# Layer two of a graph network: whole-block contexts for blocks 0 to 11, the maximum and the residual behind GpSimd's offset, half contexts for blocks 12 to 15

## The chip, the cores and the metric

The kernel runs on one core of one Trainium2 chip. The time is device microseconds for one execution, the median of several runs. Lower is better. In the text PE is TensorE (PEld its weight load), DVE is VectorE, ACT is ScalarE, POOL is GpSimd and SP is SyncE, whose queue issues the DMAs.

## The reference

Two graph layers over 128 graphs of 64 nodes with 768 features, in fp32. For one layer, with h the rows of one graph:

```
u[i,j] = h_i . (W_left h_j) for j >= i, h_i . (W_right h_j) for j < i, over sqrt(768)
att = exp(u) * adj / (row sum + 1e-10)
ctx = att @ (h @ W_lin^T + b)
h   = relu((ctx - mean) / (std(ddof=1) + 1e-3) * a + b)
```

Before layer one, h = relu(layernorm(x)); after layer two the result is x + h. What matters here is the end of layer two: the context `ctx`, its deviation, the scale by 1/(std + eps) and the row `a` (the mean is already out of it, since the weights are centred), the offset `b`, the maximum with zero, and the sum with `x`.

## The kernel before, in words

The 8192 rows are 16 blocks of 512 (8 graphs each). Each layer has two passes. Pass one (`pass_one`) makes the attention of all blocks and stores it. Pass two (`pass_two`) goes over the blocks u = 0 to 15 again: `linear(u, ...)` makes `hl` = h W_lin of block u, and the context of block u-1 is made in the midst of it, one block behind.

`linear` is a fast matrix multiplication: 15 products instead of 18 (the list `ORDER`, i = 0 to 14). For a product PE does eight matmuls of 128x256 with weights `W[l, "n"]` and a sum of token chunks; the result goes into one of four PSUM banks X, Y, Z, V. After each product the bank is added into `hl`: what comes to an `hl` part first is copied by ACT (L305), the others are added by DVE (L223). A bank that is used again has to be read out first: X takes i = 0, 2, 4, 6, 8, 10, Y takes 3, 7, 11, Z takes 1, 13, V takes 5, 9, 12, 14. `fresh` lets ACT put a bias into X, Y or V ahead of i = 0, 3, 5, 9 (L843, `AHEAD` holds the X of the next block). The eleven token sums of block u+1 (`T_SUMS`: ta, u1, u2, u0, u3, td, tb, te, tc, tg, tf) are made on POOL during block u (L223, output `ts`), from `ht` of u+1, which SP loads (`load_h`, L375) and ACT brings to relu(a h + b) in six pieces (`affine`, L382).

Everything that isn't in `ORDER` is put into numbered slots of the block by hand: `put(n, f)`. Slot 2i runs in the middle of product i, slot 2i+1 after it and after its reading; slots of 30 and more run in the next block, 30 lower. A slot sets the place of an instruction in the queue of its engine, nothing else: every engine works through its own queue in order. So `affine` stands at slots 9 to 14, the token sums at 15 to 19, 21 to 25 and 27.

The context of layer two before the change is done in halves: `finish(u, r)` for r = 0, 1, called from `linear` where `ends` names a product. It does

- `context(u, r)` (L877): 16 matmuls of 64x384 on the four 64x64 quarters of PE, into two PSUM tiles `aux` of two banks each,
- ACT: two squares with a sum (L1022) and one root (L1024),
- `inverse` (DVE, L1027 and L1028), then for each of two tiles `scaled` (DVE, L1032: context times 1/std times the row `a`; then POOL, L1035: plus the row `b`) and `done` (DVE, L1046: maximum with zero, plus `x` in the tile `xr`; two stores to the output on SP, L1048). After the second tile `residual` loads the `x` of a coming half (SP, L962).

In layer two before, `ends` puts the half (u-1, 0) behind product 0 and (u-1, 1) behind product 7 of block u, for u = 1 to 14, with the steps at slots 6, 7, 8, 11, 12 and 20, 21, 22, 30, 30. Block 15 runs as two half passes with an own placing, and `finish_last` ends the program.

In layer one (L900) most contexts are done by whole blocks: `finish_block` behind product 12. `context_block(u)` does 32 matmuls: for each of four tiles, 512 columns into a bank and 256 into another. The 512 columns of (1,1) and (1,0) go into X and Y, the rest into `aux`. As X and Y are needed again, DVE copies them into the tile `z` (L972). After that come eight squares (L983), one root for four tiles (L987, L988), the inverse (L991, L992) and the scaling on ACT (L997).

Of the kernel before, what the change touches and what calls it, by code (L numbers as in the profile page):

```python
# [13 lines left out]
ALU = mybir.AluOpType  # L14
# [3 lines left out]
def kernel(  # L18
# [12 lines left out]
    nc = tc.nc  # L31
# [33 lines left out]
    def put(slot, *fs):  # L65
        plan.setdefault(slot, []).extend(fs)
# [780 lines left out]
    def pass_two(l, aside):  # L847
        last = l == L - 1
        with (tc.tile_pool(name=f"ps_two{l}", bufs=1, space=bass.MemoryType.PSUM) as ps,
# [108 lines left out]
            def residual(u, r):  # L958
                XS[u, r] = [sp.tile([P, H], F32, name="xr", bufs=4) for _ in range(2)]
                for k in range(2):  # L960
                    for h in range(PAIR):
                        nc.sync.dma_start(XS[u, r][k][h * S:(h + 1) * S], x[u * NBB + batch(r, k, h)])  # L962

            def finish_block(u, more):

                parts = context_block(u)
                tiles = ((0, 0), (0, 1), (1, 0), (1, 1))
                zs = {t: sp.tile([P, H], F32, name="z", bufs=4) for t in tiles}
                cut = (slice(0, T), slice(T, H))

                for t in ((1, 1), (1, 0)):
                    nc.vector.tensor_copy(zs[t][:, cut[0]], parts[t][0])  # L972
                    parts[t][0] = zs[t][:, cut[0]]
                    if t == (1, 1):
                        AHEAD.append(fresh(l, 0, more))
                ss = stat.tile([P, Q, 2], F32, name="ssb", bufs=2)
                sd = stat.tile([P, Q], F32, name="sdb", bufs=2)
                rs = stat.tile([P, Q], F32, name="rsb", bufs=2)

                def squares(t):  # L980
                    junk = zs[0, t[1]]
                    for n in range(2):
                        nc.scalar.activation(junk[:, cut[n]], parts[t][n], AF.Square,  # L983
                                             accum_out=ss[:, 2 * t[0] + t[1], n:n + 1])

                def deviation():
                    nc.vector.reduce_sum(sd, ss, axis=mybir.AxisListType.X)  # L987
                    nc.scalar.activation(sd, sd, AF.Sqrt, bias=floor, scale=1.0 / (H - 1.0))  # L988

                def inverse():  # L990
                    nc.vector.tensor_scalar_add(rs, sd, EPS_LN)  # L991
                    nc.vector.reciprocal(rs, rs)  # L992

                def scaled(t):
                    by = rs[:, 2 * t[0] + t[1]:2 * t[0] + t[1] + 1]
                    for n in range(2):
                        nc.scalar.activation(zs[t][:, cut[n]], parts[t][n], AF.Copy, scale=by)  # L997
                    kept(u, *t, zs[t])

                order = ((1, 1), (1, 0), (0, 0), (0, 1))  # L1000
                for f, slots in ((squares, (25, 26, 28, 29)), (scaled, (33, 34, 35, 36))):
                    for n, t in zip(slots, order):
                        put(n, lambda f=f, t=t: f(t))
                put(30, deviation)
                put(32, inverse)

            def kept(u, r, k, z):
                for h in range(PAIR):
# [2 lines left out]
            def finish(u, r):  # L1011

                cx = context(u, r)
                zs = [sp.tile([P, H], F32, name="z", bufs=4) for _ in range(2)]
                if last and not u and not r:
                    residual(u, r)
                two = "p (n d) -> p n d"
                ss = stat.tile([P, 2], F32, name="ss", bufs=2)
                sd = stat.tile([P, 2], F32, name="sd1", bufs=2)
                rs = stat.tile([P, 2], F32, name="rs1", bufs=2)  # L1020
                for k in range(2):
                    nc.scalar.activation(zs[k].rearrange(two, n=2), cx[k], AF.Square, accum_out=ss[:, k:k + 1])  # L1022

                nc.scalar.activation(sd, ss, AF.Sqrt, bias=floor, scale=1.0 / (H - 1.0))  # L1024

                def inverse():
                    nc.vector.tensor_scalar_add(rs, sd, EPS_LN)  # L1027
                    nc.vector.reciprocal(rs, rs)  # L1028

                def scaled(k):  # L1030
                    if last:
                        nc.vector.scalar_tensor_tensor(  # L1032
                            zs[k].rearrange(two, n=2), cx[k], rs[:, k:k + 1],
                            rows["a"].rearrange(two, n=2), op0=ALU.mult, op1=ALU.mult)
                        nc.gpsimd.tensor_add(zs[k], zs[k], rows["b"])  # L1035
                        return
                    if (u, r, k) == (NB - 1, 1, 1):
                        nc.vector.tensor_scalar_mul(zs[k].rearrange(two, n=2), cx[k], rs[:, k:k + 1])
                    else:
                        nc.scalar.activation(zs[k].rearrange(two, n=2), cx[k], AF.Copy, scale=rs[:, k:k + 1])  # L1040
                    kept(u, r, k, zs[k])

                def done(k):
                    if last:
                        xs = XS[u, r]
                        nc.vector.scalar_tensor_tensor(xs[k], zs[k], 0.0, xs[k], op0=ALU.max, op1=ALU.add)  # L1046
                        for h in range(PAIR):
                            nc.sync.dma_start(out[u * NBB + batch(r, k, h)], xs[k][h * S:(h + 1) * S])  # L1048
                        if k and u + r < NB - 1 and (u, r) != (NB - 2, 0):
                            residual(u + r, 1 - r)  # L1050

                steps = [lambda f=f, k=k: f(k) for f in (scaled, done) for k in range(2)]
                return [inverse] + (steps if last else steps[:2])

# [37 lines left out]
            for u in range(NB):  # L1092
                turn = not last and u >= NB - 2
                put(4, lambda u=u: load_at(u))
                if u + 1 < NB:
                    if u:
                        load_h(2, l, u + 1)
                        put_all(9, affine(2, l, u + 1))
                    put_sums_t((2, l, u + 1), 15 if u else 21, 1, 0)
                    if not last and NB - 5 <= u < NB - 3:  # L1100
                        load_rows(1, u + 5 - NB, sp)
                        put_all(14, transpose_rows(1, u + 5 - NB, sp), 2)
                    if not last and u >= NB - 3:
                        put(2, lambda u=u: load_h(1, 1, u + 3 - NB))
                        put_all(21 if u == NB - 3 else 11, affine(1, 1, u + 3 - NB), 1 if u == NB - 3 else 3)
                    if u in aside:
                        aside[u]()
                    ends = {}
                    if u and last:
                        ends = {0: ((u - 1, 0), (6, 7, 8, 11, 12)), 7: ((u - 1, 1), (20, 21, 22, 30, 30))}  # L1110
                    elif u > NB - 3:
                        ends = {5: ((u - 1, 0), (16, 17, 18)), 11: ((u - 1, 1), (28, 29, 30))}
                    elif u:
                        ends = {12: (u - 1, None)}
                    linear(u, (0, 1), 0, ends, (0, 1) if u + 2 < NB else (0,))
                    for n in sorted(plan):
                        plan[n - 30] = plan.pop(n)
                else:
                    if turn:
                        put_token_ops(1, 0, "before")  # L1120
                        assert not idle, len(idle)
                        for n in range(RINGS - 1):
                            put(20 + 4 * n, lambda n=n: stream(1, n))
                        ends = ({1: ((u - 1, 0), (13, 14, 16)), 11: ((u - 1, 1), (34, 35, 36))},
                                {4: ((u, 0), (50, 51, 52))})
                    else:
                        last_block(u)
                        put(8, lambda: residual(u - 1, 1))
                        ends = ({0: ((u - 1, 0), (12, 13, 15, 19, 31)), 9: ((u - 1, 1), (28, 29, 30, 39, 41))},
                                {2: ((u, 0), (44, 48, 51, 61, 62))})  # L1130
                    linear(u, (0,), 0, ends[0], (1,))
                    linear(u, (1,), 30, ends[1], ())
                    for n in sorted(plan):
                        run(n)
                    for f in (finish_last if last else finish)(u, 1):
                        f()
# [72 lines left out]
```

## Time and profile before

| what | value |
|---|---|
| median of three runs | 2707.16 us (2706.79 to 2707.33) |
| the profiled execution, its own time | 2705.84 us |
| its span, first to last instruction | 2704.1 us |
| time around the span | 1.74 us |
| granted TensorE clock, mean | 0.998 |
| PE busy over the span | 2677.7 us |
| layer two, pass two, from its first product to the last context | 2223.75 to 2690.95 us |
| PE, DVE, ACT, POOL busy in one block of it (2454.94 to 2484.14, 29.20 us) | 29.20, 19.87, 13.68, 23.64 us |

In the profile, a line of the timeline gives start, duration, engine, source line, operation, tiles and count; in brackets the idle time before it and what ended it. The matmuls overlap: eight of 128x256 begin 1.727 us before the next eight. In the table by form, the numbers behind the bar are the busy time of the group and the mean time of one in ns. Times of POOL are rough.

### The profile page before, as it was taken

What the parts mean: (1) busy time and instruction counts of PE and PEld (TensorE: products, weight loads), DVE (VectorE), ACT (ScalarE), POOL (GpSimd) and SP (SyncE); (2) the same over time, 40 slices, a digit from 0 to 9 for tenths busy, and PEclk for the clock granted to TensorE, in tenths of its full rate; (3) what the DMA queues carried; (4) which work ended last, traced back from release to release, by engine and by line L of the source; (5) the groups of instructions that cost most, each with busy time, mean ns of one, the idle gap of its engine ahead of it and who ended that gap; (6) DMA issues with size and microseconds to landing.
All of it is one profiled execution on the core that took longest, in us unless ns stands there. A gap on an engine that the chain in (4) does not pass through costs nothing.

```text
span 2704.1 us, 47306 instructions
## 1 busy us (share of the span) xinstructions
PE 2677.7 (99%) x18514; PEld 2301.3 (85%) x18514; DVE 1499.1 (55%) x2456; ACT 832.4 (31%) x1617; POOL 1381.4 (51%) x1071
## 2 busy tenths in 40 slices
PE   9999999999999999999999999999999999999998
PEld 8788888888888888888788888888888888888886
DVE  7664755756647433334344545546446475666667
ACT  4032131221310254454631221221212304445443
POOL 6633244333336765566433325335244286887886
PEclk9999999999999999999999999999999999999999
DMA  8886956858765345558594956968759524655655
GB/s 272 268 309 212 289 197 208 279 202 265 244 207 181 102 143 184 166 167 255 184 284 174 317 187 212 286 191 279 229 193 301 211 79 135 182 160 159 186 154 148
DMA packets 310222, 567.81 MB, mean 210 GB/s; under 512 B 62832, under 2 KB 190064, under 8 KB 301808
## 3 DMA queue, kind: packets, MB, share of 16 engines
q1 hardware_dynamic: 309840, 564.39, 64.9%
q8 instruction: 148, 2.42, 0.4%
q14 instruction: 74, 0.61, 0.1%
q10 hardware_dynamic: 160, 0.39, 0.0%
HBM read 429.40 MB, written 135.27 MB: 209 GB/s over the span
## 4 chain that ended last, share of the span: by engine, by line
PE 96%; DVE 1%; SPq 0%; issue 0%; DMA 0%; ACT 0%; DVEq 0%; ACTq 0%
PE right L535 17%; PE X L1069 12%; PE X L535 11%; PE V L535 11%; PE Z L535 9%; PE Y L535 9%; PE V L1069 8%; PE Y L1069 6%; PE both L474 5%; PE Z L1069 4%; PE aux L877 2%; PE aux L900 1%; PE Y L900 0%; PE Z L474 0%; DVE wp L223 0%
## 5 line engine op out<-in xcount | busy, mean ns | idle before, releaser
L223 POOL TENSOR_TENSOR ts<-ht 128x512 f32<-128x512 f32 x352 | 481.6, 1374 | 172.6 <-PE X L1069 69.6
L223 POOL TENSOR_TENSOR ts<-ht,ts 128x512 f32<-128x512 f32 x192 | 252.9, 1324 | 345.7 <-PE V L535 202.1
L535 PE MATMUL right<-ts,wp 128*128 128x252 f32 (+1 forms) x1632 | 380.9, 376 | 0.6 <-DVE wp L223 0.6
L535 PEld LDWEIGHTS right<-ts,wp 128*128 128x128 f32 x1632 | 310.0, 190 | 39.5 <-DVE wp L223 1.0
L483 POOL TENSOR_TENSOR wm<-adj,tri 128x256 f32<-128x256 f32 x60 | 42.3, 728 | 490.7 <-DMA wp<-ws 274.5
L223 DVE TENSOR_TENSOR m<-m,X 128x512 f32<-128x512 f32 x160 | 105.5, 684 | 257.9 <-ACT m L305 180.2
L223 DVE TENSOR_TENSOR m<-m,right 128x504 f32<-128x504 f32 (+1 forms) x304 | 199.5, 674 | 87.8 <-PE right L535 74.1
L1069 PE MATMUL X<-room,ts 128*128 128x256 f32 x1024 | 244.0, 380 | 0.2
L535 PE MATMUL Z<-ts,wp 128*128 128x256 f32 x992 | 234.3, 379 | 0.0
L223 POOL TENSOR_TENSOR ts<-ht,ht 128x512 f32<-128x512 f32 x128 | 163.2, 1285 | 137.8 <-PE right L535 92.8
L1069 PEld LDWEIGHTS X<-room,ts 128*128 128x128 f32 x1024 | 191.7, 190 | 31.7 <-issue 1.8
L535 PEld LDWEIGHTS Z<-ts,wp 128*128 128x128 f32 x992 | 188.4, 190 | 24.9
L535 PE MATMUL X<-ts,wp 128*128 128x256 f32 x872 | 207.5, 381 | 1.9 <-DVE wp L223 1.9
L535 PE MATMUL V<-ts,wp 128*128 128x252 f32 (+1 forms) x864 | 201.6, 376 | 0.0
L305 ACT ACTIVATE m<-right 128x504 f32<-128x504 f32 (+1 forms) x64 | 36.2, 592 | 506.8 <-PE both L474 486.8
L535 PEld LDWEIGHTS X<-ts,wp 128*128 128x128 f32 x872 | 164.4, 190 | 25.5 <-POOL ts L223 2.3
L382 ACT ACTIVATE ht<-ht,b_col,a_col 128x512 f32<-128x512 f32 x192 | 141.3, 806 | 140.9 <-DMA ht<-h 140.9
L1069 PE MATMUL Y<-room,ts 128*128 128x256 f32 x768 | 182.5, 379 | 0.0
L535 PEld LDWEIGHTS V<-ts,wp 128*128 128x128 f32 x864 | 164.2, 190 | 20.4
L1069 PEld LDWEIGHTS Y<-room,ts 128*128 128x128 f32 x768 | 145.8, 190 | 20.4 <-issue 0.6
L223 DVE TENSOR_TENSOR hl<-hl,V 128x512 f32<-128x512 f32 (+1 forms) x136 | 89.2, 656 | 128.9 <-PE V L1069 118.7
L223 DVE TENSOR_TENSOR m<-m,Y 128x512 f32<-128x512 f32 x144 | 95.8, 684 | 116.0 <-PE Y L535 105.2
(225 smaller groups left out, 4866.3 us busy)
## 6 DMA issues: line engine op xcount, KB each, us to landing
wp<-ws SPq DMA_DIRECT2D x435, 512.0 KB, 6.3
ht<-h SPq DMA_DIRECT2D x62, 1536.0 KB, 8.3
h<-room SPq DMA_DIRECT2D x112, 384.0 KB, 7.1
z<-z SPq DMA_DIRECT2D x128, 192.0 KB, 3.1
ws<-wp SPq DMA_DIRECT2D x93, 256.0 KB, 4.2
xr<-in_x_dram SPq DMA_DIRECT2D x120, 192.0 KB, 3.6
out_dram<-xr SPq DMA_DIRECT2D x120, 192.0 KB, 2.6
room<-z SPq DMA_DIRECT2D x112, 192.0 KB, 5.1
```

Of the source, the lines that this page charges most:

```text
L223: (eng.tensor_add if sign == "+" else eng.tensor_sub)(o, a, b)
L305: nc.scalar.activation(to(o), p, AF.Copy, scale=1.0 if sign == "+" else -1.0)
L382: nc.scalar.activation(ht, ht, AF.Relu, bias=cols[1][:, c:c + 1], scale=cols[0][:, c:c + 1])
L474: nc.tensor.matmul(p[h * S + e:h * S + e + 32, q, e:e + 95], ht[:, c, b * S + e:b * S + e + 32], mb[:, e:e + 95], start=(c == 0), stop=(c ...
L483: nc.gpsimd.tensor_tensor(wm[:, :, k], adj[:, :, 1 - k], tri[:, k].unsqueeze(1).to_broadcast([P, Q, S]), op=ALU.mult)
L535: nc.tensor.matmul(p[:, g], wk[:, c, g * P:(g + 1) * P], tk[:, c, :].rearrange("p (b s) -> p b s", s=S)[:, :, :ns], start=(new and g == c ...
L877: nc.tensor.matmul(cx[k][i, m, :HH], at[j, q, :], hl[j, q, m * HH:(m + 1) * HH], start=True, stop=True)
L900: nc.tensor.matmul(parts[r, k][n][i], at[j, q, :], hl[j, q, cut], start=True, stop=True)
L1069: nc.tensor.matmul(p[:, n], b[t][:, c, r * P:(r + 1) * P], w[s][:, c, :], start=(i in FIRST and i not in PRELOAD and n == c == 0), stop=(c ...
```

## The change

`finish_block` now serves layer two as well. For u = 1 to 12 `ends` is {12: (u-1, None)}, so that blocks 0 to 11 get a whole-block context behind product 12. In the last layer its steps differ from those of layer one: Y is copied by ACT, not DVE; the scaling is done by DVE in two parts for each tile, with the row `a` (slots 33 to 36, in the next block 3 to 6), and POOL adds `b` to the whole tile; the maximum and the residual, now a function `added_rows`, have slots of their own, 39, 42, 44, 47 (in the next block 9, 12, 14, 17); the `x` of the next block is loaded by `residual` for both halves at slot 48 (18). For block 0 it is loaded at slot 20.

Blocks 12 to 15 keep half contexts. (12,0) and (12,1) move to behind products 9 and 14 of block 13, (13,0) and (13,1) to behind products 5 and 11 of block 14. Block 15 is as it was.

```diff
--- before.py
+++ after.py
@@ -969,7 +969,7 @@
                 cut = (slice(0, T), slice(T, H))
 
                 for t in ((1, 1), (1, 0)):
-                    nc.vector.tensor_copy(zs[t][:, cut[0]], parts[t][0])
+                    (nc.scalar.copy if last and t == (1, 0) else nc.vector.tensor_copy)(zs[t][:, cut[0]], parts[t][0])
                     parts[t][0] = zs[t][:, cut[0]]
                     if t == (1, 1):
                         AHEAD.append(fresh(l, 0, more))
@@ -993,17 +993,34 @@
 
                 def scaled(t):
                     by = rs[:, 2 * t[0] + t[1]:2 * t[0] + t[1] + 1]
+                    if last:
+                        for n in range(2):
+                            nc.vector.scalar_tensor_tensor(zs[t][:, cut[n]], parts[t][n], by, rows["a"][:, cut[n]],
+                                                           op0=ALU.mult, op1=ALU.mult)
+                        nc.gpsimd.tensor_add(zs[t], zs[t], rows["b"])
+                        return
                     for n in range(2):
                         nc.scalar.activation(zs[t][:, cut[n]], parts[t][n], AF.Copy, scale=by)
                     kept(u, *t, zs[t])
 
                 order = ((1, 1), (1, 0), (0, 0), (0, 1))
-                for f, slots in ((squares, (25, 26, 28, 29)), (scaled, (33, 34, 35, 36))):
+                steps = [(squares, (25, 26, 28, 29)), (scaled, (33, 34, 35, 36))]
+                if last:
+                    steps.append((lambda t: added_rows(u, *t, zs[t]), (39, 42, 44, 47)))
+                    for r in range(2):
+                        put(48, lambda r=r: residual(u + 1, r))
+                for f, slots in steps:
                     for n, t in zip(slots, order):
                         put(n, lambda f=f, t=t: f(t))
                 put(30, deviation)
                 put(32, inverse)
 
+            def added_rows(u, r, k, z):
+                xs = XS[u, r][k]
+                nc.vector.scalar_tensor_tensor(xs, z, 0.0, xs, op0=ALU.max, op1=ALU.add)
+                for h in range(PAIR):
+                    nc.sync.dma_start(out[u * NBB + batch(r, k, h)], xs[h * S:(h + 1) * S])
+
             def kept(u, r, k, z):
                 for h in range(PAIR):
                     nc.sync.dma_start(ROWS[u][batch(r, k, h)], z[h * S:(h + 1) * S])
@@ -1012,8 +1029,6 @@
 
                 cx = context(u, r)
                 zs = [sp.tile([P, H], F32, name="z", bufs=4) for _ in range(2)]
-                if last and not u and not r:
-                    residual(u, r)
                 two = "p (n d) -> p n d"
                 ss = stat.tile([P, 2], F32, name="ss", bufs=2)
                 sd = stat.tile([P, 2], F32, name="sd1", bufs=2)
@@ -1042,11 +1057,8 @@
 
                 def done(k):
                     if last:
-                        xs = XS[u, r]
-                        nc.vector.scalar_tensor_tensor(xs[k], zs[k], 0.0, xs[k], op0=ALU.max, op1=ALU.add)
-                        for h in range(PAIR):
-                            nc.sync.dma_start(out[u * NBB + batch(r, k, h)], xs[k][h * S:(h + 1) * S])
-                        if k and u + r < NB - 1 and (u, r) != (NB - 2, 0):
+                        added_rows(u, r, k, zs[k])
+                        if k and u + r < NB - 1 and (u, r) not in ((NB - 4, 0), (NB - 2, 0)):
                             residual(u + r, 1 - r)
 
                 steps = [lambda f=f, k=k: f(k) for f in (scaled, done) for k in range(2)]
@@ -1106,8 +1118,12 @@
                     if u in aside:
                         aside[u]()
                     ends = {}
-                    if u and last:
-                        ends = {0: ((u - 1, 0), (6, 7, 8, 11, 12)), 7: ((u - 1, 1), (20, 21, 22, 30, 30))}
+                    if last and not u:
+                        for r in range(2):
+                            put(20, lambda r=r: residual(0, r))
+                    if last and u > NB - 4:
+                        ends = ({9: ((u - 1, 0), (24, 25, 26, 29, 30)), 14: ((u - 1, 1), (34, 35, 36, 39, 40))},
+                                {5: ((u - 1, 0), (16, 17, 18, 21, 22)), 11: ((u - 1, 1), (28, 29, 30, 33, 34))})[u + 3 - NB]
                     elif u > NB - 3:
                         ends = {5: ((u - 1, 0), (16, 17, 18)), 11: ((u - 1, 1), (28, 29, 30))}
                     elif u:
```

## The prediction

> **What bounds the kernel now.** I read the busy times and the chain of the page first, then PE's timeline over one block of each layer's second pass, the busy time of each engine in one block, DVE's groups by form, and at last the few stretches where DVE and POOL work at once.
>
> ```profile
> PE 2677.7 (99%) x18514; PEld 2301.3 (85%) x18514; DVE 1499.1 (55%) x2456; ACT 832.4 (31%) x1617; POOL 1381.4 (51%) x1071
> ...
> PE 96%; DVE 1%; SPq 0%; issue 0%; DMA 0%; ACT 0%; DVEq 0%; ACTq 0%
> ```
>
> PE is the bound: work moved off another engine gains nothing; what counts is PE's own time and new waits of PE. One block of layer two (first fence) holds two half contexts, one of layer one (second) a whole one:
>
> ```profile
> 2454.94 1.89 PE L1069 MATMUL X<-room,ts 128*128 128x256 f32 x8
> 2456.76 1.52 PE L877 MATMUL aux<-hl,at 64*64 64x384 f32 x16
> 2458.21 1.99 PE L1069 MATMUL Z<-room,ts 128*128 128x256 f32 x8
> ...
> 2470.50 1.52 PE L877 MATMUL aux<-hl,at 64*64 64x384 f32 x16
> 2471.95 1.99 PE L1069 MATMUL X<-room,ht 128*128 128x256 f32 x8
> 2473.78 1.89 PE L1069 MATMUL V<-room,ht 128*128 128x256 f32 x8
> 2475.50 1.89 PE L1069 MATMUL X<-room,ts 128*128 128x256 f32 x8
> ```
>
> ```profile
> 1054.41 1.89 PE L1069 MATMUL V<-room,ts 128*128 128x256 f32 x8
> ...
> 1057.14 1.90 PE L900 MATMUL aux<-hl,at 64*64 64x256 f32 x24
> ```
>
> Products follow at 1.727 us (2473.78 to 2475.50). Layer two's block runs from 2454.94 to the next X at 2484.14: 29.20 us, no bracket with a wait. So a half costs (29.20 - 15 x 1.727) / 2 = 1.65 us. In layer one the product behind the context starts at 1030.14, one block later at 1058.97: 28.84 us with the third digit, so a whole context costs 2.94.
>
> **The gain.** Two halves 3.30, one whole 2.94: 0.36 us a block, for 12 blocks **-4.3 us**. The columns are the same (16 x 384 = 8 x 512 + 8 x 256, twice); one entry and exit less is the difference. The other edits can only lose.
>
> **The steady block (u = 2 to 12).** PE starts product i at t = 1.727 i up to 12, the context at 22.5, the next block at 28.84. A read by DVE starts 0.27 after its product. Prices:
>
> ```profile
> L1046 DVE SCALAR_TENSOR_TENSOR xr<-z,xr 128x768 f32<-128x768 f32 x48 | 91.0, 1933 | 0.0
> L1032 DVE SCALAR_TENSOR_TENSOR z<-aux,rs,a 128x768 f32<-128x768 f32 x48 | 46.5, 1010 | 0.0
> ```
>
> With both inputs in SBUF such an instruction took 0.95 at the very end, where POOL is idle, and 1.63 to 2.06 beside POOL; with PSUM, 1.01 always. The stretch 2467 to 2473 shows why: DVE waits until POOL's instruction ends, then takes 0.81; POOL's next ends 1.68 (an offset, alone 1.81) or 1.13 (a token sum, alone 1.27) after it. They take turns:
>
> ```profile
> 2467.82 3.99 DVE L1046 SCALAR_TENSOR_TENSOR xr<-z,xr 128x768 f32<-128x768 f32 x2
> ```
> ```profile
> 2465.46 3.59 POOL L1035 TENSOR_TENSOR z<-z,b 128x768 f32<-128x768 f32 x2 [3.77 <-DVE z L1032]
> 2469.01 3.93 POOL L223 TENSOR_TENSOR ts<-ht 128x512 f32<-128x512 f32 x2
> ```
>
> Scaling by parts, from these rows less the columns (0.27 per 256, by the adds of 512 at 0.69 and 256 at 0.42): 0.69 for 512 from SBUF, 0.75 from PSUM, 0.48 for 256; the next begins 0.085 before the end. DVE adds Z of i = 1 at 4.3 to 5.0, as layer one does (1066.82, block at 1062.53). Eight scalings: 4.9 to 9.1. Y of i = 3: to 9.7 (PE wants Y at 12.1). The offset of (1,1) starts at 6.0 behind its scaling, is held by the SBUF scaling of (1,0) until 6.6, ends 8.25; the second ends 10.03. Now turns: maximum (1,1) to 10.84, offset three to 12.5, maximum (1,0) to 13.3, offset four to 15.0, maximum (0,0) to **15.8**. Between them V of i = 5 is added. X of i = 8 is due at 15.54 + 0.27 = **15.8**, and PE wants X back at 17.27: two adds end at 17.1, as before (1.28 from 2474.05, PE undelayed at 2475.50). So it just fits, with about 0.1 to spare. The fourth maximum (17.0 to 19.0) delays V of i = 9 to 19.6 (wanted 20.7) and X of i = 10 to 20.8 (wanted 22.5). X is copied out at 24.5, its bias is there at 25.2 (wanted 28.84). ACT has the copy of Y, eight squares (3.96 in layer one, 1058.64 to 1062.60) and the root done by 1.5, before X of i = 0 at 1.9. POOL's sums run from 15 to 30, the next offset comes at 34.9. SP stores and loads to t = 25.5, then `ht` (7.4 to land) is there at 4.5 of the next block, wanted at 9.3. **0 us**, bound from above by the second rival.
>
> **The change back to halves (blocks 13 to 15), where nothing like it was in layer two.** Times from the start of block 14, by the same rows.
> (a) POOL reaches the offsets of (12,0) behind ten sums of block 13 (15.0 + 10 x 1.23 + two turns of 0.7): they start at -0.6, the second ends at 3.0. DVE's first maximum waits for that turn and ends at 3.8. Its two stores stand in SP's queue **ahead of `ht` of block 15**, which is issued at 5.1 and lands at 12.5 (6.9 to 8.8 in other blocks: 12.0 to 13.9). On ACT two pieces of relu wait for it, behind them the squares of (13,0), two more pieces, then the reading of X of i = 6: 12.5 + 2 x 0.72 + 2 x 0.82 + 0.3 + 2 x 0.72 + 0.6 = 17.9. PE wants X for i = 8 at 15.46: **+2.5** (2.1 to 4.0; with `ht` in time still +0.7, since the squares wait for the context at 12.0).
> (b) From i = 8 on: X read to 3.3, two scalings of (13,0) to 5.1, first offset to 6.1, a sum, second offset to 9.8 (a turn), second maximum to 11.8 (a turn), Y, V read to 13.0. PE wants V for i = 14 at 5 x 1.73 + 1.65 + 1.73 = 12.0: **+1.1** (0 to 1.3).
> (c) Context (14,0) behind the first product of block 15 (0.86) needs `aux`; the scalings of (13,1), at slots 29 and 30, come behind V of i = 14: 0.27 + 0.60 + 0.93 + 1.01 + 0.05 = 2.86: **+2.0** (before, (13,1) was done half a block earlier). Firm to 0.3: no POOL in it.
> Behind that, the maxima of (13,1) stand ahead of Y of i = 3 in DVE's queue. POOL is then at `nb`, and a DVE scalar instruction inside it was not held:
>
> ```profile
> 2666.03 2.13 POOL L922 TENSOR_SCALAR nb<-b 128x768 f32<-128x768 f32 x1
> ```
> ```profile
> 2666.94 0.16 DVE L1027 TENSOR_SCALAR rs<-sd 128x2 f32<-128x2 f32 x1
> ```
> So the maxima take 1.3 and 0.95, and Y is read in time: 0. If `nb` holds them, the second ends 2.0 + 0.81 behind the first (at 8.6 of block 15), Y is read at 11.8, and PE wants it at 9.9: up to 1.9.
> The Trainium skill, page "SBUF — State Buffer", section "SBUF: two separate sides", says that a DVE operation with two SBUF inputs and any GpSimd operation that reads SBUF lock each other out for a whole instruction. The turns above agree; `nb` reads SBUF, so by the rule the second maximum would wait for its end and the sum would be 1.9 us more. The row decides for 0, but its DVE instruction has one input, so the rule stays open there.
>
> **Sum.** -4.3 + 2.5 + 1.1 + 2.0 = **+1.3 us**. Span 2704.1 to 2705.4, own time 2705.84 to 2707.1. The median of the runs shown is 1.32 above the profiled execution: 2707.16 + 1.3 = **2708.5 us**, +0.05%. 0.2%, 5.4 us, is about what a measurement of this kernel can tell from no change.
>
> **Rivals.**
> 1. *The waits at the end are covered.* If the maximum of (12,0) meets no turn and `ht` comes early, (a) is 0.7, and (b) may be 0 where POOL is ahead: -4.3 + 0.7 + 2.0 = -1.6, 2705.6; without (c) too, 2702.9, the floor. For it: 0.1 us here and there decides (b). Against: (c) holds by DVE's order alone. 17%.
> 2. *Slower: the turns in the steady block.* Its chain of seven turns ends when X of i = 8 is due. If an SBUF scaling of 512 takes 1.1 instead of 0.69 (as the maxima do beside POOL: 1.63 for 0.95), the chain ends 0.8 later, less the 0.1 to spare, and PE waits 0.7 at i = 10 in each of 11 blocks: +7.7, 2716. It decides from 0.1 us on, and passes 0.2% at 0.4 a block. For it: no slack in the walk. Against: POOL's sums end at t = 1.1 by it, so nothing holds the scaling at 4.9. 20%.
> 3. *The change doesn't do what it says*, the whole context costs the same as two halves here: then +5.6, 2712.8. Against: the nine blocks 1030.14 to 1289.68 of layer one all take 28.84 with the same helper. 2%.
> The forecast has 61%, with 2707 to 2711 as its own range.
>
> **How the numbers follow.** The range leaves out the floor of rival 1 and the upper part of rival 2: 2704 to 2714. Faster by over 0.2% (under 2701.75) is beyond the whole gain: 2%. Slower by over 0.2% (over 2712.57): three quarters of rival 2, rival 3 and a tip of the forecast, 18%. The rest, 80%.
>
> **What would show it.** Right: blocks of 28.84 in layer two, the first X of i = 10 without a bracket; in block 14 a wait of PE at X of i = 8 released by ACT, with `ht` landing late; one at the second V; about 2 us ahead of the first context in block 15. Wrong: a wait at i = 10 in each block (rival 2), or a wait at Y of i = 7 in block 15 (`nb` holds).

## The result, and the profile after

The changed kernel takes 2713.16 us (median of 21 runs) against 2707.03 us for the kernel before (21 runs): ratio 1.0022, 95% interval 1.0015 to 1.0028. The prediction on record was 2708.5. The profiled execution took 2712.07 us with a span of 2710.3 (before: 2705.84 and 2704.1), so the difference to explain is 6.2 us. The ratios of the experiments below were measured against runs of the kernel before taken beside each experiment, so medians of different experiments compare only roughly. PE's share of the chain fell from 96% to 94%, which is waiting. The busy times and the chain of the page, kernel after:

```profile
PE 2680.2 (99%) x18514; PEld 2307.5 (85%) x18514; DVE 1503.1 (55%) x2504; ACT 840.5 (31%) x1713; POOL 1382.5 (51%) x1071
...
PE 94%; DVE 1%; POOL 1%; DMA 1%; issue 1%; SPq 0%; ACT 0%; DVEq 0%; ACTq 0%; POOLq 0%
```

To find where it lies, take the starts of the products of layer two's second pass from PE's timeline and cut the pass at the X of i = 0 of blocks 13, 14 and 15. "Sum" goes from the first product to the last context. One profiled execution of each version of the experiments below is in the table:

| kernel | to block 13 | block 13 | block 14 | block 15 | sum |
|---|---|---|---|---|---|
| before | 377.17 | 29.20 | 29.20 | 31.63 | 467.20 |
| after | 373.37 | 29.09 | 36.42 | 34.70 | 473.58 |
| tail_only | 377.18 | 29.09 | 31.98 | 35.36 | 473.61 |
| ht_early | 373.24 | 29.09 | 31.20 | 35.02 | 468.55 |
| nb_later | 373.25 | 29.09 | 31.19 | 34.08 | 467.61 |
| tail_mended | 373.23 | 29.09 | 30.71 | 34.20 | 467.23 |
| later15 | 373.27 | 29.10 | 29.91 | 36.62 | 468.90 |
| later15_max | 373.21 | 29.09 | 29.92 | 34.93 | 467.15 |
| spread | 373.22 | 29.09 | 29.30 | 33.93 | 465.54 |
| spread_b | 373.22 | 29.09 | 29.30 | 34.36 | 465.97 |
| scale_first | 373.21 | 29.09 | 29.31 | 34.02 | 465.63 |
| spread_c | 373.22 | 29.09 | 29.30 | 33.94 | 465.55 |

After minus before: -3.80 up to block 13, -0.11 in it, **+7.22 in block 14**, +3.07 in block 15; with +0.17 at the start of the pass and -0.33 behind the last context that is the 6.2. The sums are the safer measure: the first product of the pass itself starts anywhere from 2221.84 to 2227.21 us in these executions, with nothing changed ahead of it.

The whole-block context in layer two, kernel after (start, duration, engine, line, operation):

```profile
2562.10 0.65 PE L900 MATMUL Y<-hl,at 64*64 64x512 f32 x2
...
2564.84 1.35 PE L1081 MATMUL Z<-room,ts 128*128 128x256 f32 x5
```

It holds PE for 2.74 us (2562.10 to 2564.84), as in layer one. The steady block, one block of the same kernel, around the maximum of the third tile (L1020) and the X of i = 10:

```profile
2435.47 4.47 DVE L1020 SCALAR_TENSOR_TENSOR xr<-z,xr 128x768 f32<-128x768 f32 x2
...
2439.87 1.27 DVE L223 TENSOR_TENSOR hl<-hl,X 128x512 f32<-128x512 f32 x2
2441.06 2.06 DVE L1020 SCALAR_TENSOR_TENSOR xr<-z,xr 128x768 f32<-128x768 f32 x1
2441.25 1.93 PE L1081 MATMUL X<-room,ts 128*128 128x256 f32 x8
2443.02 1.24 PE L1081 MATMUL Y<-room,ts 128*128 128x256 f32 x5
```

DVE has read the X of i = 8 at 2441.14, the X of i = 10 starts 0.1 us later, and its matmuls take 1.77 instead of 1.727: a wait of 0.04 to 0.05, too short for a bracket. Eleven of these make blocks of 28.87 to 28.89 instead of 28.84, 0.5 us.

Block 14, kernel after. L1050 are the offsets of (12,0) on POOL, the first DVE line its maxima; SPq is the queue of SP, L1022 a store of `added_rows`, L375 the load of `ht`, and the bracket is the idle time before and what ended it:

```profile
2626.26 3.59 POOL L1050 TENSOR_TENSOR z<-z,b 128x768 f32<-128x768 f32 x2
...
2628.11 4.50 DVE L1020 SCALAR_TENSOR_TENSOR xr<-z,xr 128x768 f32<-128x768 f32 x2 [2.38 <-POOL z L1050]
...
2630.69 1.13 SPq L1022 DMA_DIRECT2D out_dram<-xr  x2
...
2631.93 0.52 SPq L375 DMA_DIRECT2D ht<-h  x1
...
2640.53 1.52 ACT L382 ACTIVATE ht<-ht,b_col,a_col 128x512 f32<-128x512 f32 x2 [4.61 <-DMA ht<-h]
...
2645.26 0.57 ACT L305 ACTIVATE hl<-X 128x512 f32<-128x512 f32 x1
...
2645.89 3.78 PE L1081 MATMUL X<-room,ht 128*128 128x256 f32 x8 [3.78 <-ACT hl L305]
...
2649.46 3.20 PE L1081 MATMUL V<-room,ht 128*128 128x256 f32 x8
...
2652.49 1.89 PE L1081 MATMUL X<-room,ts 128*128 128x256 f32 x8
```

The load stands behind the first two stores of (12,0), ACT stands 4.61 us for it, and PE 3.78 us for ACT (3.94 from the end of the product before, taken at 1.727, to the next start): step (a), as predicted in kind. But see the two products behind the wait: X takes 3.57 us to the next start and V 3.03, where eight matmuls take 1.727. The windows of the same stretches (wait, X, V, rest of the block; the first number behind the five engines is the granted clock):

```profile
2640.22:2645.89 5.67, 1.89 (x10) 1.33 (x8) 0.60 (x3) 5.33 (x11) 0.46 (x1) 0.95 0.91 248
2645.89:2649.46 3.57, 3.57 (x9) 2.85 (x9) 0.00 (x0) 2.36 (x4) 3.31 (x3) 0.50 0.19 69
2649.46:2652.49 3.03, 3.03 (x9) 2.45 (x8) 2.71 (x4) 0.00 (x0) 0.42 (x1) 0.57 0.00 0
2652.49:2662.80 10.31, 10.31 (x57) 7.95 (x56) 8.35 (x11) 2.37 (x6) 10.31 (x7) 1.00 0.34 82
```

The clock was halved behind the wait: 1.84 + 1.31 = 3.15 us (with the 0.10 that a product behind any wait takes longer) that nothing in the prediction has.

### The profile page after: what moved, and what is told of

Read it like the earlier page. It is cut to its first block, busy times and chain, and to the rows that moved or that the text cites. A ratio compares the mean times of both kernels' runs of the same rounds, so it can differ in the third digit from the quotient of the medians.

```text
span 2710.3 us, 47369 instructions
## 1 busy us (share of the span) xinstructions
PE 2680.2 (99%) x18514; PEld 2307.5 (85%) x18514; DVE 1503.1 (55%) x2504; ACT 840.5 (31%) x1713; POOL 1382.5 (51%) x1071
## 4 chain that ended last, share of the span: by engine, by line
PE 94%; DVE 1%; POOL 1%; DMA 1%; issue 1%; SPq 0%; ACT 0%; DVEq 0%; ACTq 0%; POOLq 0%
PE right L535 17%; PE X L1081 11%; PE X L535 11%; PE V L535 11%; PE Z L535 9%; PE Y L535 9%; PE V L1081 8%; PE Y L1081 6%; PE both L474 5%; PE Z L1081 4%; PE aux L900 2%; PE Y L900 1%; PE aux L877 1%; POOL ts L223 0%; PE Z L474 0%
## 5 line engine op out<-in xcount | busy, mean ns | idle before, releaser
L223 POOL TENSOR_TENSOR ts<-ht 128x512 f32<-128x512 f32 x352 | 460.1, 1315 | 190.9 <-PE X L1081 83.9
L223 POOL TENSOR_TENSOR ts<-ht,ts 128x512 f32<-128x512 f32 x192 | 244.2, 1279 | 349.1 <-PE V L535 205.7
```

Source lines behind the costliest of these rows:

```text
L223: (eng.tensor_add if sign == "+" else eng.tensor_sub)(o, a, b)
```

## The experiments

**Theory**: the whole-block contexts gain as worked out, and the loss sits in blocks 13 to 15 alone, in four pieces: PE waits for the late `ht` (3.94), it then runs at half clock (3.15), it waits around the context (14,0) (1.9), and for `nb` (0.85). **Rivals**: the steady block loses; or DVE and POOL are simply full at the end, and a wait that is taken away comes back.

### The end alone, and `ht` early

tail_only is the kernel before, with half contexts everywhere, and only the new places in blocks 13 and 14:

```diff
+                    if last and u > NB - 4:
+                        ends = ({9: ((u - 1, 0), (24, 25, 26, 29, 30)), 14: ((u - 1, 1), (34, 35, 36, 39, 40))},
+                                {5: ((u - 1, 0), (16, 17, 18, 21, 22)), 11: ((u - 1, 1), (28, 29, 30, 33, 34))})[u + 3 - NB]
+                    elif u and last:
```

> The kernel before, with half contexts everywhere, and only the new places of the halves in blocks 13 and 14 (behind products 9 and 14, 5 and 11). Theory (the loss sits at the change back to halves: the load of ht of block 15 stands behind the stores of (12,0), PE waits 3.8 us, then runs at half pace, and context (14,0) waits 1.9 us): nothing is gained and the whole loss stays, +9 to +10.5 us against the kernel before, ratio 1.0033 to 1.0039. Rival (the loss comes from the whole-block contexts of blocks 0 to 11, whose maxima and scalings crowd DVE and POOL): no change, ratio 0.9995 to 1.0005.

Measured: 2714.14 us, ratio 1.0030 (1.0019 to 1.0040), less than the expected 1.0033 to 1.0039, which lie inside the interval. In the table, "to block 13" is as before (377.18) and blocks 13 to 15 lose 6.4 us, where after loses 10.2 in them. So the new places at the end make the larger part of the loss without any whole-block context, and the rival falls; but they do not make all of it. tail_only, the offsets of (12,0) on POOL, the load of `ht`, and PE behind it:

```profile
2626.77 3.58 POOL L1035 TENSOR_TENSOR z<-z,b 128x768 f32<-128x768 f32 x2 [1.06 <-DVE z L1032]
...
2632.43 0.53 SPq L375 DMA_DIRECT2D ht<-h  x1
...
2646.74 1.99 PE L1069 MATMUL X<-room,ht 128*128 128x256 f32 x8 [1.14 <-ACT hl L305]
```

Block 14 starts at 2629.87 here and at 2626.38 in after. POOL is at the offsets 3.1 us ahead of the block (0.1 in after, where the four offsets of the whole-block context of block 11 hold POOL until 2612.44, ahead of the sums of block 13), `ht` is issued 2.6 us into it (5.6 in after), PE waited 1.14 for it, and the clock stayed at full, against the expectation: block 14 lasts 31.98, not 36.42.

ht_early is the changed kernel, with one load put into block 13, ahead of the stores:

```diff
                     if u:
-                        load_h(2, l, u + 1)
+                        if not (last and u == NB - 2):
+                            load_h(2, l, u + 1)
+                        if last and u == NB - 3:
+                            put(20, lambda u=u: load_h(2, l, u + 2))
```

> The changed kernel, with the load of ht of block 15 at slot 20 of block 13, ahead of the stores of (12,0) in SP's queue. Theory: ht lands before its relu is due, PE's wait at X of i = 8 in block 14 falls from 3.85 us to 0.7 (the squares of (13,0) still stand ahead), no product after it runs at half pace, so 3.1 + 3.1 us go; the wait at V of i = 14 that I had forecast may come back, up to 1.1: 5.2 to 6.3 us less than the changed kernel, about as the kernel before, ratio 0.9998 to 1.0004. Rival (the order on ACT and DVE makes the wait, and the load only shows first): block 14 stays over 34 us, ratio 1.0018 to 1.0025.

Measured: 2708.11, ratio 1.0002 (0.9993 to 1.0011), 5.05 us under the median of after, and 5.03 in the pass: by the ratio as the theory said, by the difference just under its 5.2 to 6.3. PE's two waits in block 14 of ht_early, and the maximum on DVE that makes the second:

```profile
2642.91 1.99 PE L1081 MATMUL X<-room,ht 128*128 128x256 f32 x8 [0.36 <-ACT hl L305]
...
2652.87 2.00 DVE L1020 SCALAR_TENSOR_TENSOR xr<-z,xr 128x768 f32<-128x768 f32 x1 [1.71 <-POOL z L1050]
...
2656.22 1.97 PE L1081 MATMUL V<-room,ts 128*128 128x256 f32 x8 [1.03 <-DVE hl L223]
```

The wait of 3.78 is down to 0.36, the half clock is gone (X takes 1.83 to the next start), and **the wait (b) at V of i = 14 has come out**: 1.03 in the bracket, 1.19 from start to start. In after it measured 0.03, because the half clock had stretched the two products before it by more than 1.1. One load moved for one engine's sake is worth 5.0 us, and uncovers 1.2 of another wait.

### Does the half clock follow from the wait?

held_pe is the kernel before with idle copies of one column on ACT ahead of the reading of X of i = 6, more of them from block to block, so that PE stands longer and longer:

```diff
+                    if last and i == 6:
+                        for _ in range({2: 16, 4: 20, 6: 24, 8: 28, 10: 32, 12: 36}.get(u, 0)):
+                            nc.scalar.copy(held, eps_in)
```

> The kernel before, with 16, 20, 24, 28, 32, 36 idle copies of one column on ACT ahead of reading X of i = 6 in blocks 2, 4, 6, 8, 10, 12 of layer two: PE waits at i = 8, longer from block to block, some 1 to 6 us. Nothing else is in its way. Theory (a wait of PE over some limit between 1.0 and 3.8 us halves the granted clock for a while): after the short waits a product of eight matmuls takes 1.73 us, after the long ones 3.4 to 3.6, for about 6.6 us from the first matmul, which costs about 3.1 us on top of the wait. Rival (the slow products of block 14 come from what else went on there, DMAs or DVE): 1.73 us after every wait.

Measured, one run: 2731.54 us. PE stood 0.86, 1.75, 2.64, 3.53, 4.42 and 5.32 us (from the end of the context, 1.45 behind its start, to the next product). Half pace followed the waits of 2.64, 4.42 and 5.32, and not those of 0.86, 1.75 and **3.53**. So neither of the two theories holds as it stands: the half pace came without any other change (against the rival), but length alone doesn't decide. And it cost 1.7 us each time (1.5 behind the longest wait), not the 3.1 expected. held_again repeats two lengths six times each:

```diff
-                        for _ in range({2: 16, 4: 20, 6: 24, 8: 28, 10: 32, 12: 36}.get(u, 0)):
+                        for _ in range((0, 24, 28)[0 if not 0 < u < 13 else 1 + (u - 1) % 2]):
```

> The kernel before, with 24 idle copies of one column on ACT ahead of the reading of X of i = 6 in blocks 1, 3, 5, 7, 9, 11 and 28 in blocks 2, 4, 6, 8, 10, 12: PE stands for 2.6 and 3.5 us, twelve times. Theory (whether the products behind such a wait run at half pace depends on where the wait falls in a window that runs on by itself): some waits of each length are followed by eight products of some 3.3 us instead of 1.73, others of the same length are not; time 2707 plus 12 x 2.2 plus 1.6 for each such wait, 2735 to 2748. Rival (a fixed length from which it happens): all waits of 3.5 us are followed by the half pace, and none or all of 2.6 us.

Measured, one run: 2759.85 us (the expectation set 2.2 us for a wait; they are 2.64 and 3.53, 37 us for the twelve, and with ten halvings at 1.7 that is the 54 us by which the span grew). After all six waits of 3.53 and after four of six of 2.64 PE ran at half pace. Two waits of the same length in held_again, first one without, then one with it:

```profile
2472.56 2.00 PE L1070 MATMUL X<-room,ht 128*128 128x256 f32 x8 [2.57 <-ACT hl L305]
2474.39 1.89 PE L1070 MATMUL V<-room,ht 128*128 128x256 f32 x8
...
2538.68 3.33 PE L1070 MATMUL X<-room,ht 128*128 128x256 f32 x8 [2.57 <-ACT hl L305]
2541.80 2.29 PE L1070 MATMUL V<-room,ht 128*128 128x256 f32 x8
```

Whenever it came in held_again, X and V together were longer by 1.69 us, in nine cases of ten (1.55 in the tenth), however the loss was split between them (1.29 + 0.40 in the case shown, 0.38 + 1.31 in another; the 0.10 that a product behind a context takes longer anyway is left out): half the clock for some 3.4 us.

What decides can be read from the granted clock of these traces. Within each execution the stretches of half clock begin at whole multiples of 3.413 us from one another, and each lasts one such window (in after 6.83 us, two). PE's waits don't shift this grid. Add up the idle time of PE, as the profile has it, in each window of the pass, for all fourteen traces: all 15 windows with 1.98 us or more of idle time are followed by a window at half clock, and none of the others, of which the longest has 1.87. held_pe, the wait of 2.64 (its window, and the one behind it) and that of 3.53 (its two windows, and the one behind them); behind the busy time of PE stands the granted clock:

```profile
2417.71:2421.12 3.41, 0.84 (x9) 1.00 0.83 211
2421.12:2424.53 3.41, 3.41 (x9) 0.50 1.04 272
2479.15:2482.56 3.41, 1.83 (x18) 1.00 0.63 157
2482.56:2485.98 3.41, 1.54 (x7) 1.00 0.94 253
2485.98:2489.39 3.41, 3.41 (x18) 1.00 1.00 341
```

The shorter wait lies in one window, idle for 2.57 us of it; the longer one is cut in two by a boundary, 1.58 and 1.87. So what decides is where the wait falls in these windows, as the theory of held_again has it. In after the window ahead of the half clock was idle for 3.16 us; PE still stood in the first 0.62 us of the window at half clock, and a second one followed, while the other windows at half clock in the pass had at most 0.38 idle and stood alone. How many windows a wait costs can therefore differ from one execution to the next; the medians of after and before differ by 6.1 us, the profiled executions by 6.2.

The Trainium skill, page "TensorE: Matmul & The Clock Gate", section "Part 1: The HAM clock gate (the "warmup" mystery)", describes half the clock after an idle window of about 3.4 us, until a busy one of the same length has passed, with windows that run freely. The windows of 3.413 us agree; but they need not be idle throughout, 1.98 us were enough. Its advice against idle gaps over about 3.4 us is too mild here: gaps of 2.57 behind a context did it four times in six, and in a run below one of 2.73 behind ordinary products did.

### `nb`

nb_later is ht_early with one slot changed, `nb` (POOL) at 36 instead of 6:

```diff
-                put(6, lambda: nc.gpsimd.tensor_scalar_mul(rows["-b"], rows["b"], -1.0))
+                put(36, lambda: nc.gpsimd.tensor_scalar_mul(rows["-b"], rows["b"], -1.0))
```

> The change with the load of ht(15) early, and nb at slot 36 instead of 6 of block 15. Theory (nb on POOL holds the second maximum of (13,1) on DVE, and this makes PE wait at Y of i = 7): the wait of 0.85 us there goes, and the second maximum of (13,1) takes 0.95 to 1.1 us instead of 1.6. Rival (the maximum is only late because its queue is late): the wait stays at 0.7 to 0.9.

Block 15 of after: the two maxima of (13,1) on DVE, `nb` on POOL, the reading of Y behind the maxima, and PE, which wants Y for i = 7:

```profile
2669.35 3.44 DVE L1020 SCALAR_TENSOR_TENSOR xr<-z,xr 128x768 f32<-128x768 f32 x2
...
2670.44 2.85 POOL L922 TENSOR_SCALAR nb<-b 128x768 f32<-128x768 f32 x1
...
2672.71 0.41 DVE L223 TENSOR_TENSOR hl<-hl,Y 128x256 f32<-128x256 f32 x1
...
2673.27 1.10 PE L1081 MATMUL Y<-room,ts 128*128 128x256 f32 x4 [0.69 <-DVE hl L223]
```

The same maxima in nb_later:

```profile
2665.25 2.79 DVE L1020 SCALAR_TENSOR_TENSOR xr<-z,xr 128x768 f32<-128x768 f32 x2
```

Measured: 2707.59 us (one run), pass 467.61. The pair takes 2.79 instead of 3.44, PE's product ahead of Y 1.07 instead of 1.72 (0.864 undisturbed), and block 15 is 0.94 shorter than in ht_early. The theory holds: `nb` was the cause, for three quarters of that wait; 0.21 stays, and that this is the first maximum sharing with POOL's offset is argued, not shown. By these lines neither held the other throughout: in after the second maximum ends at 2672.79, before `nb` ends (2673.28), 0.65 later than without it, while `nb` takes 2.85 instead of the 2.13 before. POOL's spans are rough, but the rule weighed in the prediction (whoever is first holds the other for a whole instruction) would have made 1.9 us.

### Can the waits at the end be got rid of?

tail_mended is ht_early with (13,0) behind product 6 and the steps of (13,1) spread otherwise:

```diff
-   {5: ((u - 1, 0), (16, 17, 18, 21, 22)), 11: ((u - 1, 1), (28, 29, 30, 33, 34))}
+   {6: ((u - 1, 0), (18, 19, 20, 23, 24)), 11: ((u - 1, 1), (26, 26, 26, 37, 37))}
```

> As ht_early, and (13,0) behind product 6, so that X of i = 6 is read ahead of its squares; the scalings of (13,1) at slot 26 instead of 29 and 30, so that context (14,0) finds aux free; the maxima of (13,1) behind Y of i = 3 of block 15. Theory: all three waits go (0.7, 1.9, 0.8 us) and the gain of 12 x 0.36 less 0.5 us is left: 2703 to 2704 where the kernel before is 2707, ratio 0.9984 to 0.9990. Rival (DVE is so full in these blocks that a wait moved away comes back at another bank): ratio 0.9995 to 1.0005.

Measured: 2707.63, ratio 0.9998 (0.9989 to 1.0007), pass 467.23, the same as before. **The theory missed**, and the rival's ratio came true: of the 5.4 us that ht_early loses in blocks 14 and 15 (31.20 + 35.02 against 29.20 + 31.63) only 1.3 went. The wait around the context (14,0) fell from 1.9 to 1.1 and that for `nb` to nothing, but V of i = 14 of block 14 waits 1.3 (1.2 before), 0.7 has come at the context (14,1) and 0.2 more at V of i = 14 of block 15 (in the expectations below this wait is put down to Z of i = 13; it is V of i = 14, behind the reading of V of i = 12). tail_mended, the maxima of (13,0) beside POOL's sums:

```profile
2651.41 4.50 DVE L1020 SCALAR_TENSOR_TENSOR xr<-z,xr 128x768 f32<-128x768 f32 x2
...
2653.11 3.92 POOL L223 TENSOR_TENSOR ts<-ht 128x512 f32<-128x512 f32 x2
...
2656.65 1.97 PE L1081 MATMUL V<-room,ts 128*128 128x256 f32 x8 [1.17 <-DVE hl L223]
```

The two maxima, 1.9 us alone, hold DVE for 4.50 as they take turns with POOL, and the reading of V stands behind them. later15 therefore puts the second one behind that reading, and the context (14,0) two products later; the loads of `x` go ahead of the maxima, `nb` to 36. later15_max also moves the maxima of the steady block (second diff):

```diff
-   {5: ((u - 1, 0), (16, 17, 18, 21, 22)), 11: ((u - 1, 1), (28, 29, 30, 33, 34))}
+   {5: ((u - 1, 0), (16, 17, 18, 21, 25)), 11: ((u - 1, 1), (28, 29, 30, 33, 34))}
-   {0: ((u - 1, 0), (12, 13, 15, 19, 31)), 9: ((u - 1, 1), (28, 29, 30, 39, 41))}
+   {2: ((u - 1, 0), (13, 14, 16, 20, 31)), 9: ((u - 1, 1), (28, 29, 30, 39, 41))}
```
```diff
-   steps.append((lambda t: added_rows(u, *t, zs[t]), (39, 42, 44, 47)))
+   steps.append((lambda t: added_rows(u, *t, zs[t]), (39, 42, 47, 49)))
```

> The change with the load of ht(15) early, and with the places of blocks 14 and 15 set by DVE's queue: the second maximum of (13,0) behind the reading of V of i = 12, the context (14,0) behind product 2 of block 15 instead of 0, the x of (13,1) and (14,0) loaded ahead of the maxima, nb at slot 36. Theory (the 3 us of the last three blocks are waits for DVE at three places, each with its own queue in front, and all can be got out of the way at once): the wait at V of i = 14 (1.1), the two around the context (14,0) (1.9), those at Y of i = 7 (0.85) and Z of i = 13 (0.7) of block 15 go, 4 us in all; the pass lasts 464 to 465 us against 467.2 before, ratio 0.9985 to 0.9993. Rival (DVE and POOL are simply full in these blocks, a wait that is moved away comes back elsewhere, as the run before this one suggests): 0.9996 to 1.0004, with 3 us or more of waits in the trace at other places.

> The same, with the third and the fourth maximum of the whole-block contexts at slots 47 and 49 instead of 44 and 47, and the load of the next x at slot 50. Theory (the 0.05 us at X of i = 10 in each of 11 steady blocks are the third maximum ahead of the reading of X of i = 8): these waits go, the block is 28.84 instead of 28.88, 0.5 us in all, ratio 0.0002 below that of the run beside it. Rival (the four turns of maximum and offset only move, and a later bank waits): blocks of 28.88 or more, ratio the same or up to 0.0005 above.

Measured: later15 2708.10, ratio 1.0002 (0.9993 to 1.0010); later15_max 2708.28, ratio 1.0003 (0.9994 to 1.0012). The rival again. The waits named are gone from block 14 (but for 0.5 at X of i = 8), and one of 2.7 has come in block 15. later15, POOL's offset (L1050), the maxima of (13,1) that wait for it, and PE behind the reading of Y:

```profile
2660.49 3.56 POOL L1050 TENSOR_TENSOR z<-z,b 128x768 f32<-128x768 f32 x2
...
2662.32 3.42 DVE L1020 SCALAR_TENSOR_TENSOR xr<-z,xr 128x768 f32<-128x768 f32 x2 [3.73 <-POOL z L1050]
...
2666.22 1.71 PE L1081 MATMUL Y<-room,ts 128*128 128x256 f32 x4 [2.73 <-DVE hl L223]
```

and the same product in later15_max:

```profile
2667.79 1.10 PE L1081 MATMUL Y<-room,ts 128*128 128x256 f32 x4 [2.74 <-DVE hl L223]
```

DVE stands 3.73 us at the head of its queue for an offset that POOL reaches only behind its sums. The same wait of PE is followed by half pace in the one (1.71) and not in the other (1.10): in later15 all of its 2.73 lie in one window of the clock, in later15_max a boundary cuts it into 1.60 and 1.14. Block 15 is 36.62 and 34.93, a difference of 1.69, the stretch measured above. As for the steady block, in later15_max the waits at i = 10 are gone and eleven of twelve blocks take 28.83 or 28.84; block 8 takes 29.18 (29.17 in spread), with a wait of 0.34 at X of i = 10, whose cause stays open. So "to block 13" falls by no more than 0.16 against after, and the time by nothing that shows.

spread and spread_b put the maxima of (13,1) behind the readings too, at slots 7 and 10, or 8 and 11, of block 15, and (13,0) behind product 6 (the line of later15_max, then that of spread and that of spread_b):

```diff
-   {5: ((u - 1, 0), (16, 17, 18, 21, 25)), 11: ((u - 1, 1), (28, 29, 30, 33, 34))}
+   {6: ((u - 1, 0), (18, 19, 20, 23, 25)), 11: ((u - 1, 1), (28, 29, 30, 37, 40))}
+   {6: ((u - 1, 0), (18, 19, 20, 25, 27)), 11: ((u - 1, 1), (28, 29, 30, 38, 41))}
```

> As the run later15_max, with (13,0) behind product 6 (second maximum behind the reading of V of i = 12), and the two maxima of (13,1) at slots 7 and 10 of block 15 instead of 3 and 4, so that DVE does not stand at the first for POOL's offset (3.7 us in that run, PE 2.9 of them) with the reading of Y of i = 3 behind it; the x of (14,1) is loaded at slot 12. Theory (the waits come back only where an instruction that waits for POOL stands ahead of a reading, so with the maxima behind the readings the gain of the whole-block contexts comes through): the wait of 2.9 us goes, what is left is under 1 us in all, the pass lasts 463 to 464 us against 467.2 before, ratio 0.9984 to 0.9991. Rival (DVE and POOL are full in these blocks, whatever the order): again 2 to 4 us of waits, pass 465.5 to 467.5, ratio 0.9995 to 1.0003.

> The same, with the maxima of (13,0) at slots 25 and 27 of block 14 and those of (13,1) at 8 and 11 of block 15. Theory: the second maximum of (13,0) then stands ahead of the scalings of (13,1) and makes these late by 0.5 to 1 us, which the later context (14,0) covers; pass 463 to 464.5 us, ratio 0.9984 to 0.9992. Rival: 0.9995 to 1.0003.

Measured: spread 2705.16, ratio 0.9994 (0.9985 to 1.0003), pass 465.54; spread_b 2706.04, ratio 0.9996 (0.9987 to 1.0005), pass 465.97. **Block 14 is now free of waits** (29.30 with its two half contexts, 29.20 before). Block 15 still loses 2.3 us in spread, 2.7 in spread_b. Here I had expected less: the pass of spread stands at the lower end of the rival's 465.5 to 467.5, and the ratio of spread_b is inside the rival's range too. The last two aim at what is left (spread, then scale_first, which also has both scalings of (14,0) at slot 14, then spread_c):

```diff
-   11: ((u - 1, 1), (28, 29, 30, 37, 40))
+   11: ((u - 1, 1), (28, 29, 30, 38, 46))
+   11: ((u - 1, 1), (28, 29, 30, 38, 41))
```

> As the run spread, with the second maximum of (13,1) behind the scalings of (14,0) in block 15 (slots 8 and 16 instead of 7 and 10, both scalings at 14, the x of (14,1) at 18). In the run spread 2.3 us were left, both in block 15 and both behind the two maxima of (13,1) in a row on DVE: 1.4 at V of i = 9, which waits for the reading of V of i = 5, and 0.9 in the context (14,1), which waits for the scalings of (14,0). Theory (only these orders cost, not the work): both waits go, the pass lasts 462 to 463 us against 467.2 before, ratio 0.9983 to 0.9990. Rival (a wait comes back at another place): pass 464 to 466, ratio 0.9993 to 1.0.

> As the run spread, with the maxima of (13,1) at slots 8 and 11 of block 15, one ahead of the reading of V of i = 5 and one behind it. Theory: the wait at V of i = 9 goes, that in the context (14,1) falls from 0.9 to 0.2 to 0.4; pass 462 to 463.2 us, ratio 0.9983 to 0.9991. Rival: pass 464 to 466, ratio 0.9993 to 1.0.

Measured: scale_first 2705.05, ratio 0.9992 (0.9983 to 1.0001), pass 465.63; spread_c **2704.05, ratio 0.9991** (0.9982 to 1.0000), pass 465.55. Against spread nothing is won in the pass: the wait ahead of V of i = 9 fell from 1.4 to 0.5, and the one in the context (14,1) rose from 0.9 to 1.95 and 1.75. By the pass the rival (464 to 466, a wait comes back at another place) was right both times. spread_c, the scalings of (14,0), the context that needs their PSUM banks, and the next product:

```profile
2669.61 1.94 DVE L1047 SCALAR_TENSOR_TENSOR z<-aux,rs,a 128x768 f32<-128x768 f32 x2
2670.68 2.43 PE L877 MATMUL aux<-hl,at 64*64 64x384 f32 x16 [0.67 <-DVE z L1047]
...
2673.04 1.13 PE L1081 MATMUL X<-room,ts 128*128 128x256 f32 x4
```

The context (14,0) was moved two products back, (14,1) was not, so (14,1) now comes before its banks are free. A later place for (14,1) was not tried. What the profiled executions show is that 1.7 us of the 4 us of gain come through to the end of the pass (467.20 to 465.5), and spread_c, picked as the best of nine such variants, is below the kernel before by an interval that ends at no change; that it is faster is not shown.

## Why the prediction was near, and where it failed

Its time was 4.7 us too low, a little more than the gain it was about; the signs of nearly all steps were right. That 2713.16 lies inside its 2704 to 2714 is in part luck: it is outside the forecast's own 2707 to 2711 and above the 2712.57 that the prediction gives 18% to pass, mostly for rivals 2 and 3, which are not what happened.

- **The gain, -4.3**: measured -3.80 up to block 13, -0.11 in it. The 0.36 per block was exact (28.84 is the block where nothing waits). What is missing is the step "the steady block: 0 us, with about 0.1 to spare": the third maximum ended at 16.0 instead of 15.8 and the two adds at 17.2 instead of 17.1, and PE waits 0.04 to 0.05 in eleven blocks, 0.5 us; in later15_max, with the third maximum behind the reading, this goes. This is rival 2 in its smallest form, and a walk that ends with 0.1 to spare should have been given that.
- **(a), +2.5**: measured 3.94, just inside its 2.1 to 4.0. `ht` was issued at 5.55 (5.1 predicted) and ACT began on it 8.6 later (7.4 to land). ht_early shows the mechanism, the load behind the stores, by its absence; in tail_only the same load is 3 us earlier and the wait falls to 1.14.
- **The step that failed** is none of the sum's terms; it is that (a) was priced as its wait alone. The wait brought 3.15 us of half clock, the largest part of the error. The profile of before shows a mean clock of 0.998 and no wait of that length in this pass, and the prediction did not name the granted clock at all. Its range (2704 to 2714) holds the time without having a term for it. What the runs showed in its place: PE stood for 3.16 us of one window of 3.413 us, and two windows at half clock followed.
- **(b), +1.1**: 0.03 in after, 1.19 as soon as `ht` was early. The step was right and was hidden by the half clock ahead of it.
- **(c), +2.0**: 1.92.
- **`nb`, 0 by a row with one input**: the wait at Y of i = 7, which the prediction had named as a sign that `nb` holds, came: 0.85, of which `nb` makes 0.65, between the row and the 1.9 of the skill's rule. The row was about another kind of instruction, and the prediction said so; the middle would have been the better value. V of i = 14 in block 15 waits 0.35 more, not foreseen.

By these terms: 1.44 + 3.15 + 0.85 + 0.35 + 0.5 - 1.07 - 0.1 = 5.1 us, against 2712.07 - 2707.1 = 4.97 between the profiled executions; the -0.11 of block 13 and the +0.17 and -0.33 at the ends of the pass are not in them.

Of the rivals, 1 (covered waits at the end) is what ht_early brings about in part, and 3 (no gain) falls with the 28.84. The floor that rival 1 gives, 2702.9, is the gain alone, with (a) at nothing; with its own 0.7 for (a) it is 2703.6.

## What to carry to other kernels

Where PE is the bound, price a predicted wait of PE of more than some two microseconds with the chance of a stretch of half clock on top, 1.7 us here for each, and look for the granted clock in the windows behind the wait; taking away the one long wait was worth 5 us, moving many short ones about 1 to 3. When an order of work is changed for the steady state, work out the change-over at its end first, queue by queue: here one load behind two stores cost more (5.0 us, with the half clock) than twelve blocks gained (3.8). And before a wait is moved, ask what stands behind the instruction that waits: an in-order queue with an instruction at its head that waits for another engine passes the wait to everything behind it.

## What the runs showed of the hardware that I had not expected

- TensorE's clock halves behind waits of 2.6 us and more, not always: 0 of 2 waits up to 1.75 us in held_pe, 5 of 7 of 2.64 and 6 of 7 of 3.53 in held_pe and held_again together. The idle time in one of the windows of 3.413 us separates them: 1.98 us and more in 15 windows, always followed by half clock, 1.87 and less never. In a stretch of half clock the matmuls of 128x256 start 0.43 us apart instead of 0.216.
- A maximum with two SBUF inputs on DVE and a TENSOR_SCALAR on POOL slow each other, by POOL's rough spans without either standing for the whole of the other: 0.65 us more for the pair of maxima, 0.7 for `nb`.
